# GRU layer with residual, one core: the input weights as one load over 128 rows each, x turned by each fourth column, and a new order of early loads

## The chip, the cores and the metric

The kernel runs on one core of a Trainium2 chip. The metric is the device time of one execution in microseconds (us). The time of the kernel before is the median of three runs; a few per mille of it are at stake here, so times are given to a hundredth.

## What is computed

x is 64 sequences of 128 steps with 512 features; the state h has 512 features. Each gate has a weight of 1024 rows: the first 512 meet x (the input weights), the last 512 meet the state (the state weights). All is float32.

```
def step(h, inp):
    x_t, prop = inp
    comb = jnp.concatenate([x_t, h], axis=-1)
    z = jax.nn.sigmoid(comb @ Wz + bz)
    r = jax.nn.sigmoid(comb @ Wr + br)
    comb2 = jnp.concatenate([x_t, r * h], axis=-1)
    h_cand = jnp.tanh(comb2 @ Wh + bh)
    h_new = (1.0 - z) * h + z * h_cand
    h_next = jnp.where(prop, jnp.tanh(h_new @ Wp + bp), h_new)
    return (h_next, h_new)
```

prop is true at each fourth step but the last. The output is x plus h_new of every step.

## The kernel before

**Layout.** The batch is cut into two halves h of 32. A tile of x or of the state has 128 partitions: partition 32q+b holds, for sequence b of a half, the quarter q (128 features) of the vector. VectorE's transpose works on 32x32 blocks. `join_x` (L254 to 263) turns one step of x, so that partition 32q+e then holds, in slot k, feature 128q+32k+e for all sequences. The weights stand to match: `load_w` (L98 to 103) loads rows 128q+32k to 128q+32k+31 to partitions 32q to 32q+31, slot k, with one DMA for each q, that is 4 DMAs of 32 partitions, on two queues by turns (SyncE's, SP, and ScalarE's, ACT). The input weights lie in one tile, wx; the state weights in wh[0] to wh[2] (r, z, h) and wp.

**Two kinds of products on TensorE.** All are recorded at L218. The products of the state with wh and wp are the recurrence: step t needs step t-1. The products of x with wx (`fill`) depend on no state; they stand in a queue of units, from which the code takes a counted number at set places of each step (`PLACES`, `HEAD`, `TAIL`, L613 to 620), so that TensorE has work while the gates are computed. Steps 0 to 3 take plain products. Later steps are done in groups of four by a scheme with fewer products, for which GpSimd (POOL) forms sums of rows of x (`sum_raw12` and the like, L330 to 359) and of parts of wx (`sum_outer`, `sum_inner`), and joins the results into cp (L564 to 570).

**One step** (`half`, L817 to 906; both halves run interleaved): gate r; sigmoid of r on ScalarE; r*h on VectorE (L834) and its turn (L835, recorded at L247); gate z; sigmoid of z; keep = (z-1)*h on VectorE (L850); gate h with r*h; tanh; two VectorE operations (L873, L882) and the turn of the new state (L883), with which the next step begins. `seed` copies the x part into a gate's accumulator (ScalarE, L394). `join(t, duo, u, n)` (L724) turns steps of x at two places of a step: n=0 stands behind the turn of r*h of the second half (L841), n=1 behind keep (L853). The loop repeats every 8 steps; u counts them, and duo is the round.

**The start** (L120 to 142 and L632 to 674), in the order written: steps 0 and 1 of x (step 1 on GpSimd's queue), wx for r in two parts, the biases, wx for z, wx for h, the initial state; 48 small products that only keep TensorE busy (`idle`, L633); turns of steps 0 and 1; the x products of r for both steps; then steps 2 and 3 of x and wh of r; the x products of z, then wh of z; the x products of h, then wh of h; then x for steps 4 to 11, wp and more x (`later_loads`). Then 6 units of step 2, and the recurrence.

Each queue issues in order. An issue of SP or ACT takes one of eight completion semaphores by turns, and waits until the load that had it eight places earlier in the common order of both queues has landed. On ACT an issue that waits also holds up the copies and sigmoids behind it. In the program built from it, TensorE's first product with a weight waits for all parts of that weight.

Of the kernel before, what the change touches and what calls it, by code (L numbers as in the profile page):

```python
# [18 lines left out]
def kernel(  # L19
# [14 lines left out]
    nc = tc.nc  # L34
    B, T, D = x.shape
# [7 lines left out]
    K = D // P  # L43
# [4 lines left out]
    R, Z, H_ = range(3)  # L48
# [22 lines left out]
    wx = const.tile([P, K, 3, H], F32, name="wx")  # L71
# [10 lines left out]
    gates_in = (Wr, Wz, Wh)  # L82
# [5 lines left out]
    def part(q):  # L88
        return slice(q * V, (q + 1) * V)
# [8 lines left out]
    def load_w(wt, w, k0=0, k1=K, engs=(nc.sync, nc.sync)):  # L98
        for q in (0, 2, 1, 3):
            engs[q // 2].dma_start(  # L100
                out=wt[part(q), k0:k1, :],
                in_=w[q * P + k0 * V : q * P + k1 * V, :].rearrange("(k e) n -> e k n", e=V),
            )

    both_queues = (nc.sync, nc.scalar)
# [6 lines left out]
    def load_step(t, engs=both_queues):  # L112
        for q in (0, 2, 1, 3):
            engs[q // 2].dma_start(
                out=xr[0][part(q), t], in_=x[:, t, ts(q, J)].rearrange("(h b) u -> b h u", h=S)
            )

    software_queue = (nc.gpsimd, nc.gpsimd)

    h_init = two.tile([P, S, J], F32, tag="h", name="h_init")  # L120
    bias_x = const.tile([P, C, S, 3, J // 2], F32, name="bias_x")
    bias_p = const.tile([P, S, J], F32, name="bias_p")
    new_xr(0)
    load_step(0)
    load_w(wx[:, :, R, :], gates_in[R][:D], 0, 2, both_queues)
    load_step(1, software_queue)
    for i, b in enumerate((br, bh, bz)):
        nc.gpsimd.dma_start(out=bias_row[:, i, :], in_=b.rearrange("(o n) -> o n", o=1))
    load_w(wx[:, :, R, :], gates_in[R][:D], 2, K, both_queues)

    dummy = const.tile([1, 1], F32, name="dummy")
    nc.scalar.activation(dummy, ones[:, 0:1], AF.Sigmoid)

    for i in (Z, H_):
        load_w(wx[:, :, i, :], gates_in[i][:D], engs=both_queues)

    held = const.tile([1, 1], F32, name="held")
    nc.gpsimd.tensor_copy(held, wx[0:1, 2, R, 0:1])
    for h in range(S):
        nc.gpsimd.dma_start(  # L140
            out=h_init[:, h, :],
            in_=h0[ts(h, V), :].rearrange("b (q j) -> q b j", q=NQ),
        )

    def load_wh(i):
        load_w(wh[i], gates_in[i][D:], engs=both_queues)
# [107 lines left out]
    def join_x(g, i):  # L254
        if g * Q4 >= T:
            return
        if g not in xT:
            xT[g] = xtp.tile([P, Q4, C, P], F32, tag="xT", name=f"xT_{g}")
        src = xr[g] if g < FIRST else xs[g]
        nc.vector.transpose(  # L260
            out=xT[g][:, i].rearrange("p c (a h b) -> p h (c a) b", a=S, h=S),
            in_=src[:, i].rearrange("p h (k e) -> p h k e", k=K),
        )

    def outer(kb, nb, ka):
# [29 lines left out]
    def sum_outer(n):  # L295
        for ka in range(S):
            if n == 3:
                nc.gpsimd.tensor_sub(tw[3][:, ka], outer(1, 1, ka), outer(0, 1, ka))
            elif n == 2:
                nc.gpsimd.tensor_add(tw[2][:, ka], tw[3][:, ka], outer(0, 0, ka))  # L300
            else:
                nc.gpsimd.tensor_sub(tw[4][:, ka], outer(1, 0, ka), tw[2][:, ka])
# [27 lines left out]
    def sum_raw12(g):  # L330
        v = xT[g]
        sx[g, 12] = one.tile([P, 4, C, B], F32, tag="s12r", name=f"s12r_{g}")
        four([sx[g, 12][:, n] for n in range(4)], v[:, 0], v[:, 1])
# [19 lines left out]
    def sum_s34(g):  # L353
        v = xT[g]
        o = sx[g, "o34"] = one.tile([P, 2, 2, P], F32, tag="o34", name=f"o34_{g}")
        nc.gpsimd.tensor_sub(o[:, 0], v[:, 0:2, 0, :], v[:, 2:4, 0, :])
        nc.gpsimd.tensor_sub(o[:, 1], v[:, 0:2, 1, :], sx[g, "o12"][:, 1])
        s = sx[g, 73] = one.tile([P, 4, 2, B], F32, tag="s73", name=f"s73_{g}")
        four([s[:, n] for n in range(4)], o[:, :, 0], o[:, :, 1])
# [31 lines left out]
    def seed(i, t, h):  # L391
        if t < T:
            rows = slice(None) if i == Z else ts(h, 2 * V)
            nc.scalar.copy(  # L394
                gate_ps(i, h)[rows].rearrange("p d (c n) -> p d c n", c=C),
                G[t][rows, :, :, i, :].rearrange("p c d n -> p d c n"),
            )
# [181 lines left out]
    def outer_1(g):  # L579
        with_bias(g, 1, bias0)  # L580

    def outer_c11(g):
        add(c_block(g, 0, 0), m_(g, 1), m_(g, 2))
# [14 lines left out]
    def outer_c22(g):  # L598
        add(c_block(g, 1, 1), m_(g, 7), m_(g, 5))

    def outer_c21(g):
        add(c_block(g, 1, 0), m_(g, 7), m_(g, 4))

    def pair_left(a, p1, p2, g=1):
        with_bias(g, p2, bias0)
        add(c_block(g, a, 0), m_(g, p1), m_(g, p2))

    def pair_right(a, p1, x_, g=1):
        with_bias(g, x_, bias_x[:, 1])
        add(c_block(g, a, 1), m_(g, p1), m_(g, x_))  # L610
# [17 lines left out]
    def now(units):  # L628
        put(units)
        both(len(units))  # L630
# [7 lines left out]
    spread(scratch[3], slice(0, 2), (R, H_))  # L638
    spread(scratch[1], slice(2, 3), (Z,))
    nc.gpsimd.tensor_sub(bias_d, bias_x[:, 1], bias0)  # L640
    load_step(2)
    now(first[R][0][2:] + first[R][1][2:])
    for t in range(2):
        add_bias(t, (R,))
    for h in range(S):
        seed(R, 0, h)
    load_step(3)
    load_wh(R)
    now(sum(first[Z], []))
    for i in (1, 2):  # L650
        sum_inner(i, nc.vector, slice(0, 2))
# [72 lines left out]
    def join(t, duo, u, n):  # L724
        even, odd = FIRST + 2 * duo, FIRST + 2 * duo + 1
        if t == 1:
            join_x(1, 2 + n)
        elif t == 2:
            join_x(2, n)
        elif t == 4:  # L730
            join_x(3, 2 * n)
            join_x(3, 2 * n + 1)
        elif duo >= 0 and u in (5, 6):
            join_x(even + 2, 2 * (u - 5) + n)
        elif duo >= 1 and u in (1, 3):
            join_x(odd, u - 1 + n)

    def behind_step(t, duo, u, h_new):
        g, j = divmod(t, Q4)
        even, odd = FIRST + 2 * duo, FIRST + 2 * duo + 1  # L740
        if t == T - 7:
            pair_left(0, 1, 2, LAST)
            pair_right(0, 1, 10, LAST)
        if t == 0:
            sum_outer(2)
            sum_outer(4)
        if t == 3:
            pair_left(1, 8, 9)
            pair_right(1, 8, 11)

        if duo >= 0:
            if u == 0 and duo >= 1 and odd - 2 < LAST:
                outer_c22(odd - 2)
                outer_c21(odd - 2)
            if even * Q4 < T:
                if u == 0:
                    sum_s34(even)
                elif u == 1:
                    outer_1(even)
                    outer_c11(even)  # L760
                    sum_raw12(odd)
                elif u == 2:
                    outer_u1(even)
                    outer_5(even)
                    sum_raw4(even)
                elif u == 3:
                    outer_c12(even)
                    outer_u2(even)
                    outer_c22(even)
                    if odd < LAST:  # L770
                        sum_s12(odd)
                elif u == 4:
                    if odd < LAST:
                        sum_s34(odd)
                    outer_c21(even)
                    if odd < LAST:
                        outer_1(odd)
                elif u == 5 and odd < LAST:
                    sum_raw4(odd)
                elif u == 6 and odd < LAST:  # L780
                    outer_u1(odd)
                    outer_c11(odd)
                elif u == 7 and odd < LAST:
                    outer_5(odd)
                    outer_c12(odd)
        if duo >= -1 and (even + 2) * Q4 < T:
            if t == 2 or (u == 6 and duo >= 0):
                sum_raw12(even + 2)
            if u == 7:
                sum_s12(even + 2)  # L790
        if t < T - 1:
            nc.gpsimd.tensor_add(xr[g][:, j], xr[g][:, j], h_new)  # L792

        n = 0
        if t >= T - CHUNK:
            n = 3 if t == T - 2 else 0
        elif j == Q4 - 1:
            n = 4
        if n:
            for h in range(S):  # L800
                for q in range(NQ):
                    nc.sync.dma_start(  # L802
                        out=out[ts(h, V), t - n + 1 : t + 1, ts(q, J)],
                        in_=xr[g][part(q), j - n + 1 : j + 1, h, :],
                    )
        if j == 1 and g >= 1 and (g + 1) * Q4 < T:
            new_xr(g + 1)
            load_x(xr[g + 1], (g + 1) * Q4, Q4)
        if t in (1, 2):
            load_xs(t + 2)  # L810
        if duo >= 0:
            if u == 3:
                load_xs(odd + 2)
            elif u == 6:
                load_xs(even + 4)

    def half(h):  # L817
# [95 lines left out]
    while any(live):  # L913
        h = 0 if live[0] and (not live[1] or at[0] <= at[1]) else 1
# [46 lines left out]
```

## Time and profile before

| | |
|---|---|
| median of 3 runs | 1269.17 us (1269.16 to 1270.07) |
| the profiled execution's own time | 1271.65 us |
| its span on the core | 1269.8 us |
| TensorE products busy | 1251.8 us (99%), 25960 instructions |
| VectorE busy | 772.3 us (61%) |
| ScalarE busy | 835.7 us (66%) |
| GpSimd busy | 893.1 us (70%) |
| DMA | 60.82 MB, mean 48 GB/s |

The profile is of one execution. Its own time is 1.85 us more than its span, and 2.48 us more than the median of the runs. PE is TensorE's products, PEld its weight loads, DVE VectorE, ACT ScalarE, POOL GpSimd, SPq, ACTq and POOLq the issues of DMAs on these engines. In a row of the timeline stand start, busy time, engine, line, operation and, in brackets, how long the engine was idle before it and what ended that. In a row of stretches stand, for each engine, busy time and instructions, then the clock granted to TensorE (1.00 is full), the share of the 16 DMA engines' time that was busy, and GB/s.

### The profile page before, as it was taken

Reading aid. Unit: us, or ns where it says so; the run is one execution under the profiler, and the core shown is the slowest. Engines: PE = TensorE matmul, PEld = TensorE weight load, DVE = VectorE, ACT = ScalarE, POOL = GpSimd, SP = SyncE. Lnnn points to the kernel's source line nnn. Section 1 sums busy time; section 2 is a strip of 40 time slices with the busy share of each in tenths; the row PEclk is TensorE's granted clock in tenths of the full one; section 3 lists DMA queues with packets and bytes.
Section 4 is the critical chain, followed back from the end, with each engine's and each line's share of the span. In section 5 each row is a group of like instructions: output and inputs, shape, how many; then the busy total and the mean of one; then the engine's idle time right before and its main releaser. Section 6 shows DMA issues by size and latency. Waiting matters only on the chain.

```text
span 1269.8 us, 60717 instructions
## 1 busy us (share of the span) xinstructions
PE 1251.8 (99%) x25960; PEld 1164.5 (92%) x25960; DVE 772.3 (61%) x2165; ACT 835.7 (66%) x2685; POOL 893.1 (70%) x1036
## 2 busy tenths in 40 slices
PE   7999999999999999999999999999999999999997
PEld 4898899999999999999999999999999999999875
DVE  3565666666666666666666666666666666665554
ACT  1466666666666666667666667666666766667665
POOL 3889767787677777767787677786777687677530
PEclk9999999999999999999999999999999999999999
DMA  9401222111121111212101121111111112111010
GB/s 212 109 15 48 53 52 51 38 32 43 51 53 36 43 46 36 53 38 62 38 24 52 53 52 37 36 44 45 52 37 49 40 36 53 44 45 36 9 46 19
DMA packets 113172, 60.82 MB, mean 48 GB/s; under 512 B 12968, under 2 KB 109224, under 8 KB 112904
## 3 DMA queue, kind: packets, MB, share of 16 engines
q1 hardware_dynamic: 110148, 53.26, 16.3%
q8 instruction: 205, 3.36, 1.2%
q10 hardware_dynamic: 2372, 3.41, 1.2%
q14 instruction: 63, 0.52, 0.1%
q0 software_dynamic: 384, 0.27, 0.1%
HBM read 40.11 MB, written 16.78 MB: 45 GB/s over the span
## 4 chain that ended last, share of the span: by engine, by line
PE 92%; POOL 2%; DMA 2%; issue 1%; ACT 1%; DVE 1%; SPq 0%; ACTq 0%; POOLq 0%; DVEq 0%
PE rec L218 42%; PE rec_z L218 15%; PE scratch_r L218 13%; PE scratch_q L218 10%; PE scratch_a L218 5%; PE scratch_y L218 4%; PE scratch_x L218 4%; DMA wx<-in_L_cond_Wh_dram 1%; POOL cp L565 1%; POOL mb L570 1%; DMA wh<-in_L_cond_Wr_dram 0%; DMA xr<-in_x_dram 0%; DMA wx<-in_L_cond_Wr_dram 0%; ACT rec_z L244 0%; SPq L802 0%
## 5 line engine op out<-in xcount | busy, mean ns | idle before, releaser
L218 PE MATMUL rec<-wh,rhT 128*32 128x256 f32 x4096 | 375.4, 379 | 0.1
L218 PE MATMUL rec<-wh,hT 128*32 128x256 f32 x3072 | 281.5, 379 | 1.3 <-DVE hT L247 1.3
L218 PE MATMUL rec_z<-wh,hT 128*32 128x256 f32 x3072 | 281.7, 379 | 0.1
L218 PEld LDWEIGHTS rec<-wh,rhT 128*32 128x32 f32 x4096 | 250.1, 110 | 19.2 <-ACT scratch_r L244 0.5
L244 ACT ACTIVATE scratch_r<-rec 64x128 f32<-64x128 f32 x512 | 128.0, 250 | 137.6 <-PE rec L218 64.0
L394 ACT COPY rec<-cp 64x256 f32<-64x256 f32 x512 | 189.8, 371 | 27.1 <-DMA xr<-in_x_dram 7.6
L218 PEld LDWEIGHTS rec_z<-wh,hT 128*32 128x32 f32 x3072 | 192.4, 110 | 9.7 <-ACT rec_z L394 0.6
L218 PEld LDWEIGHTS rec<-wh,hT 128*32 128x32 f32 x3072 | 186.4, 110 | 14.7 <-ACT c L244 3.2
L244 ACT ACTIVATE rec_z<-rec_z 64x128 f32<-64x128 f32 x512 | 128.0, 250 | 98.1 <-PE rec_z L218 86.0
L244 ACT ACTIVATE c<-rec 64x128 f32<-64x128 f32 x512 | 139.3, 272 | 60.1 <-PE rec L218 48.6
L792 POOL TENSOR_TENSOR xr<-xr,h 128x256 f32<-128x256 f32 x127 | 92.9, 732 | 93.0 <-DVE h L882 93.0
L565 POOL TENSOR_TENSOR mb<-mb,mb 128x768 f32<-128x768 f32 x58 | 106.2, 1830 | 67.0 <-DVE mb L531 67.0
L565 POOL TENSOR_TENSOR cp<-mb,mb 128x768 f32<-128x768 f32 x76 | 138.8, 1827 | 8.1 <-DVE mb L531 4.4
L565 POOL TENSOR_TENSOR cp<-mb 128x768 f32<-128x768 f32 x46 | 84.2, 1831 | 56.9 <-ACT rec_z L394 55.5
L850 DVE SCALAR_TENSOR_TENSOR keep<-rec_z,h 128x256 f32<-128x256 f32 x96 | 40.8, 425 | 133.7 <-ACT rec_z L244 127.4
L218 PE MATMUL scratch_r<-tw,s 128*32 128x192 f32 x928 | 120.9, 326 | 0.0
L504 ACT COPY cq<-scratch_q 128x384 f32<-128x384 f32 x212 | 102.1, 482 | 19.7 <-PE scratch_q L218 18.3
L521 DVE TENSOR_TENSOR cx<-scratch_r,cx 128x384 f32<-128x384 f32 x106 | 59.1, 557 | 81.4 <-PE scratch_r L218 70.1
L218 PE MATMUL scratch_q<-tt,s 128*32 128x192 f32 x928 | 103.6, 326 | 0.0
L527 DVE TENSOR_TENSOR mb<-scratch_q,cx 128x384 f32<-128x384 f32 x106 | 59.1, 557 | 57.8 <-ACT cq L504 57.6
L834 DVE TENSOR_TENSOR rh<-scratch_r,h 128x128 f32<-128x128 f32 x192 | 56.0, 292 | 60.3 <-ACT scratch_r L244 60.3
L218 PE MATMUL rec<-wh,hpT 128*32 128x256 f32 x992 | 91.5, 379 | 0.1
(184 smaller groups left out, 3819.9 us busy)
## 6 DMA issues: line engine op xcount, KB each, us to landing
out_dram<-xr SPq DMA_DIRECT2D x249, 64.0 KB, 1.8
xr<-in_x_dram SPq DMA_DIRECT2D x248, 64.0 KB, 2.1
xs<-in_x_dram SPq DMA_DIRECT2D x240, 64.0 KB, 2.2
wp<-in_L_cond_Wp_dram SPq DMA_DIRECT2D x4, 256.0 KB, 5.0
wx<-in_L_cond_Wr_dram SPq DMA_DIRECT2D x4, 128.0 KB, 3.6
wx<-in_L_cond_Wr_dram ACTq DMA_DIRECT2D x4, 128.0 KB, 4.1
wx<-in_L_cond_Wz_dram ACTq DMA_DIRECT2D x2, 256.0 KB, 5.9
wx<-in_L_cond_Wz_dram SPq DMA_DIRECT2D x2, 256.0 KB, 6.6
```

What stands on the lines that cost most here:

```text
L218: nc.tensor.matmul(ps[part(2 * h + c)], lhsT=left, rhs=rhs(c), start=start, stop=True, skip_group_check=True,)
L244: nc.scalar.activation(dst[ts(d, 2 * V)], gate_ps(i, h)[ts(h, 2 * V), d, :], func)
L394: nc.scalar.copy(gate_ps(i, h)[rows].rearrange("p d (c n) -> p d c n", c=C), G[t][rows, :, :, i, :].rearrange("p c d n -> p d c n"),)
L504: nc.scalar.copy(c[:, :nm], ps[:, :nm])
L521: nc.vector.tensor_add(T2[what][:, :nm], r_ps[:, :nm], T2[what][:, :nm])
L527: nc.vector.tensor_add(blocks(1, 1), runs(q_ps[:, :nm]), runs(T2[what][:, :nm]))
L565: nc.gpsimd.tensor_add(dst, a, b)
L570: nc.gpsimd.tensor_add(m, m, v.unsqueeze(1).to_broadcast([P, 2, 3 * J]))
L792: nc.gpsimd.tensor_add(xr[g][:, j], xr[g][:, j], h_new)
L834: nc.vector.tensor_mul(rh[:, h, :], r_, h_old[:, h, :])
L850: nc.vector.scalar_tensor_tensor(out=keep, in0=z, scalar=1.0, in1=h_old, op0=ALU.subtract, op1=ALU.mult)
```

## The change

- wx is loaded by a new `load_wx`: one DMA over 128 partitions for each gate, two for r (slots 0 and 1, then 2 and 3), all on SP's queue. Partition p holds in slot k row 4p+k of the weight.
- `join_x` reads x to match: within a quarter, the 32 columns e of slot k are each fourth column, 4e+k, where they were 32 neighbours.
- Step 1 of x goes from GpSimd's queue to ACT's. Step 2 (all on ACT's) is issued ahead of the initial state, where it stood behind the first x products of r. Step 3 goes to ACT's queue.
- wh of r takes the place in the order that step 2 had, ahead of step 3, where it stood behind step 3.
- In the loop the joins with n=1 go; their turns stand with n=0, behind the turn of r*h, in part a step later: u=5 one turn, u=6 one, u=7 two; and u=1 two, u=2 one, u=3 one. Before it was two in each of u=5, 6, 1 and 3, one at each place.
- The load of the next even group of x follows at u=7, where it followed at u=6.

```diff
+    def load_wx(i, k0, k1):
+        nc.sync.dma_start(
+            out=wx[:, k0:k1, i, :],
+            in_=gates_in[i][:D].rearrange("(p k) n -> p k n", k=K)[:, k0:k1],
+        )
...
     load_step(0)
-    load_w(wx[:, :, R, :], gates_in[R][:D], 0, 2, both_queues)
-    load_step(1, software_queue)
+    load_wx(R, 0, 2)
+    load_step(1, (nc.scalar, nc.scalar))
...
-    load_w(wx[:, :, R, :], gates_in[R][:D], 2, K, both_queues)
+    load_wx(R, 2, K)
...
     for i in (Z, H_):
-        load_w(wx[:, :, i, :], gates_in[i][:D], engs=both_queues)
+        load_wx(i, 0, K)
+    load_step(2, (nc.scalar, nc.scalar))
...
-            in_=src[:, i].rearrange("p h (k e) -> p h k e", k=K),
+            in_=src[:, i].rearrange("p h (e k) -> p h k e", k=K),
...
-    load_step(2)
+    load_wh(R)
     now(first[R][0][2:] + first[R][1][2:])
...
-    load_step(3)
-    load_wh(R)
+    load_step(3, (nc.scalar, nc.scalar))
...
-        elif duo >= 0 and u in (5, 6):
-            join_x(even + 2, 2 * (u - 5) + n)
-        elif duo >= 1 and u in (1, 3):
-            join_x(odd, u - 1 + n)
+        elif n == 0:
+            if duo >= 0 and u in (5, 6):
+                join_x(even + 2, u - 5)
+            elif duo >= 0 and u == 7:
+                join_x(even + 2, 2)
+                join_x(even + 2, 3)
+            elif duo >= 1 and u == 1:
+                join_x(odd, 0)
+                join_x(odd, 1)
+            elif duo >= 1 and u in (2, 3):
+                join_x(odd, u)
...
-            elif u == 6:
+            elif u == 7:
                 load_xs(even + 4)
```

More of the change, by code (lines that the diff above doesn't have):

```diff
@@ L116, in load_step @@
             )
-    software_queue = (nc.gpsimd, nc.gpsimd)
+    def load_wx(i, k0, k1):
[3 more added lines that the diff above has]
+        )
     h_init = two.tile([P, S, J], F32, tag="h", name="h_init")
```

## The prediction

> **What bounds the kernel now.** The stretches of the windows view come first, because an average hides that this kernel has three parts.
>
> ```profile
> span 1269.8 us, 60717 instructions
> 0.00:28.50 28.50, 20.32 (x304) 10.69 (x304) 11.52 (x31) 3.53 (x8) 8.39 (x19) 1.00 0.89 210
> 28.50:60.00 31.50, 31.42 (x590) 25.64 (x594) 15.62 (x46) 14.82 (x49) 28.85 (x29) 0.95 0.53 122
> 60.00:110.00 50.00, 48.91 (x1059) 46.52 (x1053) 28.80 (x79) 29.48 (x92) 41.23 (x48) 1.00 0.18 45
> 510.00:710.00 200.00, 200.00 (x4204) 190.49 (x4199) 126.43 (x355) 137.48 (x442) 145.19 (x168) 1.00 0.18 47
> 710.00:910.00 200.00, 200.00 (x4219) 191.39 (x4215) 126.08 (x353) 136.93 (x440) 147.33 (x177) 1.00 0.17 45
> ```
>
> The first column after the stretch is its length, the next TensorE's busy time. From 510 to 910 TensorE is busy for 400.00 of 400.00 us at clock 1.00: nothing that another engine gains there can shorten it. The change leaves the products and their order alone (as many of them, line for line, in both programs). So the loop can only lose. At the start it is otherwise: 8.2 us of 28.50 are idle, and the DMA engines are busy for 0.89 of their time. The waits of TensorE and its timeline name the holes.
>
> ```profile
> PE rec L218 <- DMA wh<-in_L_cond_Wr_dram: 3.2, 1, 3.2
> PE scratch_r L218 <- DMA xr<-in_x_dram: 1.9, 1, 1.9
> PE scratch_a L218 <- DVE xT L260: 1.0, 1, 1.0
> ...
> 15.23 1.94 PE L218 MATMUL scratch_a<-wx,xT 128*32 128x256 f32 x32
> 19.12 1.93 PE L218 MATMUL scratch_r<-wx,xT 128*32 128x256 f32 x32 [1.95 <-DMA xr<-in_x_dram]
> ...
> 22.57 2.80 PE L218 MATMUL scratch_q<-wx,xT 128*32 128x256 f32 x48
> 28.58 2.74 PE L218 MATMUL rec<-wh,hT_init 128*32 128x256 f32 x28 [3.21 <-DMA wh<-in_L_cond_Wr_dram]
> ```
>
> In order: the x products of z end at 17.17; those of h begin at 19.12, when wx of h is there (scratch_r is their accumulator; the x named as releaser was issued together with it); they and six units of step 2 run to 25.37; then TensorE stands until 28.58 for r's state weights (wh of r). The recurrence begins there, and everything after it moves with it.
>
> The hole has a second price, in the clock.
>
> ```profile
> 29.80:33.20 3.40, 3.40 (x40) 2.23 (x34) 0.60 (x2) 1.42 (x5) 3.24 (x5) 0.53 1.08 216
> 33.20:36.00 2.80, 2.80 (x60) 2.08 (x55) 1.24 (x4) 1.06 (x4) 2.80 (x3) 1.00 0.57 108
> ```
>
> Right after the hole the granted clock is 0.53 for 3.4 us, and only 40 products run. At the rate of the next stretch (60 in 2.80 us) 40 take 1.87 us: 1.5 us lost.
>
> **The change part by part.**
>
> *wh of r sooner.* Its loads were issued late.
>
> ```profile
> 11.55 2.52 SPq L114 DMA_DIRECT2D xr<-in_x_dram  x4
> 17.55 2.38 SPq L100 DMA_DIRECT2D wh<-in_L_cond_Wr_dram  x2
> ...
> 15.02 4.19 ACTq L114 DMA_DIRECT2D xr<-in_x_dram  x2
> 19.30 0.49 ACTq L114 DMA_DIRECT2D xr<-in_x_dram  x1
> 20.31 2.32 ACTq L100 DMA_DIRECT2D wh<-in_L_cond_Wr_dram  x2
> ...
> 15.00:18.00 3.00, 2.17 (x42) 1.26 (x32) 2.79 (x9) 0.00 (x0) 0.00 (x0) 1.00 1.00 230
> 18.00:21.00 3.00, 1.88 (x36) 1.44 (x40) 0.24 (x2) 0.74 (x2) 0.00 (x0) 1.00 0.63 135
> ```
>
> They stood behind steps 2 and 3 of x, each of which waits for a semaphore of a load still under way, and the DMA engines fell from 230 to 135 GB/s meanwhile. In the new order SP's two parts wait only for the second part of wx of r and for the first part of step 2, ACT's two for the last part of step 1 and for wx of z. All four waits end before wx of h has landed, so wh of r lies in the queue when the engines come free. Its 1 MB at 230 GB/s takes 4.6 us behind wx of h (about 18.9): landed near 23.5, while TensorE is at work until 25.37. I take the whole 3.2 us as gone; cover left 1.9 us, and beyond it each us late costs one us. What waits behind: on ACT the copies that seed r, the third part of step 3 (which now waits for all of wx of h), the seed of z, wh of z and of h, then the first sigmoid of r; all have until 25 to 34, as below.
>
> *The half clock.* If TensorE goes on from 25.37 without a hole, the 1.5 us go too. Bounds: 0 (another hole brings it) and 1.6 (the stretch's 3.40 x 0.47).
>
> *wx as one load of 128 partitions, all from SP; step 1 of x on ACT's queue.* As many bytes and rows of 2 KB; 12 issues of about 0.3 to 0.5 us become 4 on SP. No row shows an input weight loaded so. The stretches bound what could be gained:
>
> ```profile
> 1.50:3.00 1.50, 1.50 (x20) 0.61 (x16) 0.00 (x0) 0.00 (x0) 1.50 (x3) 1.00 0.50 106
> 3.00:4.50 1.50, 1.50 (x20) 0.53 (x16) 0.29 (x1) 0.12 (x1) 1.50 (x4) 1.00 0.89 259
> 12.00:15.00 3.00, 2.45 (x48) 1.43 (x44) 2.29 (x6) 0.00 (x0) 0.74 (x1) 1.00 1.08 199
> ```
>
> Between 106 and 259 GB/s there is room for a steeper start; from 3 us on the engines are full. The best case for wx of h is that nearly all of the wait of 1.9 us vanishes, say 1.7 (more can't, since z's x products end at 17.17); the worst, that half of step 2, now ahead of it (0.06 MB, 0.3 us at 230 GB/s), and slower work of one queue make it 1.0 later. I take 0.4 us earlier. The wait of 1.0 us for step 1 is worth nothing either way: z's weights and then h's are waited for behind it.
>
> *x turned by each fourth column.* No row has such a read.
>
> ```profile
> L260 DVE STREAM_TRANSPOSE xT<-xs 128x256 f32<-128x256 f32 x120 | 51.2, 429 | 2.2 <-issue 0.4
> L306 DVE TENSOR_TENSOR d<-wx 128x768 f32<-128x768 f32 x2 | 1.8, 932 | 0.0
> ```
>
> Bounds: 0.43 us as now, and 0.93 us, as a pass over three times the columns. I take 0.43, the same instruction. In the start the turns of steps 0, 2 and 3 lie under weights still in flight; in the loop the next rows say what hides them.
>
> *Joins behind the turn of r\*h.* The tightest place is u=7, where two turns come together:
>
> ```profile
> 692.53 0.31 DVE L247 STREAM_TRANSPOSE rhT<-rh 128x128 f32<-128x128 f32 x1
> 693.88 0.42 DVE L850 SCALAR_TENSOR_TENSOR keep<-rec_z,h 128x256 f32<-128x256 f32 x1 [1.04 <-ACT rec_z L244]
> 694.51 0.29 DVE L873 TENSOR_TENSOR rec_z<-c,rec_z 128x128 f32<-128x128 f32 x1 [0.21 <-ACT c L244]
> ...
> 695.24 0.31 DVE L247 STREAM_TRANSPOSE hT<-h 128x128 f32<-128x128 f32 x1
> 695.97 0.41 PE L218 MATMUL rec<-wp,hT 128*32 128x256 f32 x2
> ```
>
> VectorE is idle for 1.04 us ahead of keep, so two turns of 0.43 fit and keep is not late. Cost 0. If turns grow, 0.21 us of idle time ahead of L873 and 0.42 us between the end of hT (695.55) and its use (695.97) come on top: 1.67 us for two, 0.83 each, before TensorE waits.
>
> *Behind the start.* If the recurrence begins 5 us sooner, what is late next?
>
> ```profile
> 35.44 0.41 PE L218 MATMUL rec_z<-wh,hT_init 128*32 128x256 f32 x2
> 39.56 1.29 PE rec L218 x24
> ...
> 40.61 0.46 POOL L325 TENSOR_TENSOR s12r<-xT 128x128 f32<-128x128 f32 x1 [2.02 <-DVE xT L260]
> 67.97 0.46 POOL L325 TENSOR_TENSOR s12r<-xT 128x128 f32<-128x128 f32 x1 [7.43 <-PE scratch_r L218]
> ```
>
> wh of z is wanted at 35.44 - 5 = 30, wh of h at 34.5. Each is 1 MB: after 23.5, step 3 and these at 4.6 us each land near 28 and 33. GpSimd's start may stay where it is: it has 2.0 and 7.4 us to give up to 67.97, where TensorE releases it. So the gain is kept.
>
> The sum: 3.2 + 1.5 + 0.4 = 5.1 us. Against the profiled execution: 1271.65 - 5.1 = 1266.55; its time is 2.48 above the median, and I take the same terms for the other runs: 1269.17 - 5.1 = **1264.1 us**.
>
> **The rivals.**
>
> 1. *The half clock comes elsewhere.* TensorE still stands between 17.17 and about 18.7; were it to stand for 3 us there, half speed would fall on h's x products. Against: before, 1.9 us there brought none. Then 3.2 + 0.4 = 3.6: 1265.6. The Trainium skill, TensorE: Matmul & The Clock Gate, Part 1, "What's actually happening", says that the clock is halved after an idle window of about 3.4 us that runs freely, so the same hole may or may not cost; the trace agrees in the length of the slow stretch (3.4 us at 0.53), and by that rule the chance of this rival is not small.
>
> 2. *wh of r takes bandwidth from wx of h.* If the queues share, ACT's half (0.5 MB, 2.2 us at 230) goes beside it: h's products begin 2.2 - 0.4 = 1.8 us later at 20.9, the hole ahead of them grows to 3.7 and brings the half clock there. The recurrence begins at 25.37 + 1.8 + 1.5 = 28.7, 0.1 late, and 1.5 are saved behind it: gain 1.4, 1267.8. Against it:
>
> ```profile
> wh<-in_L_cond_Wr_dram SPq DMA_DIRECT2D x1, 256.0 KB, 4.3
> xr<-in_x_dram ACTq DMA_DIRECT2D x2, 32.0 KB, 4.0
> ```
>
> Issued together (19.3 to 20.3), two loads of 32 KB on ACT's queue took as long as one of 256 KB on SP's: they land in order of issue, not by shares of the queues.
>
> 3. *Slower: the turns by each fourth column stall the loop.* The point is 0.83 us a turn (above). At 1.25 us, three times now, a pair at u=7 is 2.5 - 1.67 = 0.83 us too long; 120 turns are 15 rounds, so 12.5 us: 1264.1 + 12.5 = 1276.6. Faster turns to slower at (5.1/15 + 1.67)/2 = 1.0 us. The Trainium skill, SBUF — State Buffer, "Door 1: The DMA port swizzle", speaks for it: memory lines are 16 bytes, and each access that crosses to a new line pays; each fourth float does so every time. No row here has such a read.
>
> **How the numbers follow.** Forecast 0.60; rival 1 0.15; rival 2 0.12; rival 3 0.09; that the change brings almost nothing, because ACT's waits hold wh of r back as before, 0.04 (near 1269). A measurement of this kernel can tell about 0.2% from no change, 2.5 us: faster is below 1266.6. The forecast and rival 1 lie below it, as does 0.02 of rival 2: faster 0.77; same 0.10 + 0.04 = 0.14; slower 0.09. The range takes the best of all terms, 3.2 + 1.6 + 1.7 = 6.5 (1262.7), and the worst without rival 3: 3.2 + 0 - 1.0 = 2.2 (1267.0).
>
> **What would show it.** The first product of rec with wh at 24.2 to 25.6 and no wait for wh of r; clock 1.00 from 25 to 36; the wait ahead of scratch_r 1 to 2 us; turns at 0.43 us; 200 of 200 us busy from 510 on. It is wrong if wx of h lands after 20, if the clock falls anywhere, or if TensorE is idle in the loop behind hT.

## The result, and the profile after

After: **1265.95 us** median (1264.16 to 1266.38, 7 runs); before in the same session 1269.17 (1268.55 to 1272.09, 7 runs). The ratio is 0.9967, 95% interval 0.9955 to 0.9978: faster by 3.2 us, inside the range 1262.7 to 1267.0 and 1.85 us above the forecast. The profiled execution took 1266.30 us, its span 1264.5. The gain is 3.2 of the 5.1 us that were forecast; the experiments show that it comes for the most part from another place than the prediction said.

The stretches of after, columns as before:

```profile
span 1264.5 us, 60718 instructions
0.00:28.50 28.50, 24.61 (x372) 12.06 (x374) 12.76 (x33) 5.28 (x14) 6.97 (x16) 0.94 0.88 237
28.50:60.00 31.50, 31.50 (x656) 24.21 (x650) 19.42 (x51) 15.94 (x52) 28.60 (x28) 1.00 0.44 109
60.00:110.00 50.00, 48.93 (x1050) 44.16 (x1043) 29.93 (x80) 30.33 (x96) 46.20 (x50) 1.00 0.15 39
510.00:710.00 200.00, 200.00 (x4206) 192.26 (x4201) 132.08 (x353) 136.57 (x439) 144.61 (x167) 1.00 0.17 46
710.00:910.00 200.00, 200.00 (x4218) 192.26 (x4213) 130.66 (x352) 136.64 (x440) 148.65 (x173) 1.00 0.16 42
```

The loop is as it was (200 of 200 us, as many products to within two). From 28.5 to 60 the clock is 1.00 in place of 0.95. In the first stretch it is 0.94 in place of 1.00: the half clock has moved there. The timeline of TensorE in after:

```profile
5.24 0.39 PE L213 MATMUL rec_z<-zeros 128*32 128x512 bf16 x4
6.83 1.07 PE L223 MATMUL scratch_q<-wx,xT 128*32 128x256 f32 x16 [1.20 <-DMA wx<-in_L_cond_Wr_dram]
9.38 1.07 PE L223 MATMUL scratch_a<-wx,xT 128*32 128x256 f32 x16 [1.49 <-DVE xT L265]
10.39 1.06 PE L195 MATMUL scratch_x<-tt,ones 1*32 1x512 f32 x8
11.27 0.94 PE L195 MATMUL scratch_r<-tt,ones 1*32 1x256 f32 x8
12.14 1.94 PE L223 MATMUL scratch_q<-wx,xT 128*32 128x256 f32 x16
...
15.20 1.90 PE L223 MATMUL scratch_q<-wx,xT 128*32 128x256 f32 x32
...
18.65 1.90 PE L223 MATMUL scratch_r<-wx,xT 128*32 128x256 f32 x32
...
24.70 1.93 PE L223 MATMUL rec<-wh,hT_init 128*32 128x256 f32 x28
```

Rec begins at 24.70 in place of 28.58. Neither h's x products nor rec wait: from 9.38 on TensorE runs without a hole. But its clock is halved from 11.4 to 14.8 (16 products take 1.94 us there, at full clock 1.07), and so TensorE itself has become the bound of the start. From the first product of rec to the end: 1264.5 - 24.70 = 1239.8 us; before 1269.8 - 28.58 = 1241.2, of which 1.5 were the half clock at 29.8. So 3.9 + 1.4 = 5.3 us were gained in the profiles.

The loads show why nothing waits for weights any more behind 9.38. Stretches of before:

```profile
6.00:9.00 3.00, 1.65 (x28) 0.78 (x28) 0.45 (x1) 0.00 (x0) 1.52 (x3) 1.00 1.09 248
9.00:12.00 3.00, 3.00 (x52) 1.16 (x44) 0.00 (x0) 0.92 (x3) 0.26 (x1) 1.00 1.07 240
```

The same stretches of after, and a later one in which state weights arrive:

```profile
6.00:9.00 3.00, 1.07 (x16) 0.50 (x16) 0.30 (x1) 0.00 (x0) 0.28 (x2) 1.00 1.07 385
9.00:12.00 3.00, 2.62 (x32) 0.82 (x32) 0.33 (x1) 0.49 (x2) 1.23 (x2) 0.90 1.02 344
18.00:21.00 3.00, 3.00 (x60) 1.68 (x56) 2.93 (x10) 0.00 (x0) 0.00 (x0) 1.00 0.87 185
```

At an engine share of 1.0 to 1.1 in both, the load over 128 partitions moves 344 to 385 GB/s, the loads over 32 partitions 240 to 248. These are the rates of these stretches: from 24 to 27, where before has only loads over 32 partitions under way, it reaches 298 at a share of 1.03. wx of h has landed at 16.5; before at 18.9.

The price is on VectorE. The turns of x in the loop, by shape, in after:

```profile
L265 DVE STREAM_TRANSPOSE xT<-xs 128x256 f32<-128x256 f32 x120 | 74.4, 641 | 1.9
```

641 ns in place of 429, within the bounds given and under the stall point of 0.83 us.

### The profile page after: what moved, and what is told of

It reads as the page before. It is cut to its first block, busy times and chain, and to the rows that moved or that the text cites. A ratio compares the mean times of both kernels' runs of the same rounds, so it can differ in the third digit from the quotient of the medians.

```text
span 1264.5 us, 60718 instructions
## 1 busy us (share of the span) xinstructions
PE 1250.6 (99%) x25960; PEld 1161.0 (92%) x25960; DVE 803.9 (64%) x2165; ACT 835.2 (66%) x2685; POOL 891.1 (70%) x1032
## 4 chain that ended last, share of the span: by engine, by line
PE 94%; POOL 2%; issue 1%; DMA 1%; ACT 1%; DVE 1%; SPq 0%; ACTq 0%; POOLq 0%; DVEq 0%
PE rec L223 42%; PE rec_z L223 16%; PE scratch_r L223 13%; PE scratch_q L223 10%; PE scratch_a L223 5%; PE scratch_x L223 4%; PE scratch_y L223 4%; DMA xr<-in_x_dram 1%; POOL cp L570 1%; POOL mb L575 1%; ACT rec_z L249 0%; SPq L813 0%; POOL xr L803 0%; ACT c L249 0%; DVE rec_z L884 0%
## 5 line engine op out<-in xcount | busy, mean ns | idle before, releaser
L223 PEld LDWEIGHTS rec<-wh,hT 128*32 128x32 f32 x3072 | 186.2, 110 | 14.6 <-ACT c L249 2.7
```

The lines of the kernel that those rows point to most:

```text
L223: nc.tensor.matmul(ps[part(2 * h + c)], lhsT=left, rhs=rhs(c), start=start, stop=True, skip_group_check=True,)
```

## The experiments

All twelve in one table. They ran in three groups, e1 to e4, e5 to e8 and e9 to e12, each with before beside it, so kernels of different groups are best compared by their ratios. The first product of rec and the time from there to the end of the span are those of the profiled execution; medians are of 6 to 12 runs, ratios against before in the same group (1270.3 to 1270.7 us).

| kernel | median (range) us | ratio, 95% interval | first rec | rest |
|---|---|---|---|---|
| before | 1269.17 (1268.55 to 1272.09) | 1 | 28.58 | 1241.2 |
| after | 1265.95 (1264.16 to 1266.38) | 0.9967, 0.9955 to 0.9978 | 24.70 | 1239.8 |
| e12_control (after again) | 1265.71 (1264.83 to 1269.60) | 0.9966, 0.9955 to 0.9978 | 23.52 | 1239.9 |
| e1_order_only | 1270.66 (1269.74 to 1271.79) | 1.0002, 0.9994 to 1.0011 | 28.87 | 1239.5 |
| e5_order_behind_copies | 1269.41 (1267.91 to 1270.41) | 0.9989, 0.9981 to 0.9998 | 26.21 | 1239.7 |
| e2_wx_only | 1268.86 (1267.45 to 1272.24) | 0.9993, 0.9983 to 1.0003 | 26.16 | 1242.3 |
| e6_joins_as_before | 1270.60 (1269.14 to 1273.38) | 1.0006, 0.9996 to 1.0016 | 26.43 | 1242.4 |
| e11_no_order | 1266.21 (1265.07 to 1270.05) | 0.9973, 0.9964 to 0.9982 | 25.13 | 1239.6 |
| e3_step1_both | 1269.20 (1267.09 to 1270.46) | 0.9988, 0.9979 to 0.9997 | 27.13 | 1239.9 |
| e4_idle | 1264.99 (1264.30 to 1270.47) | 0.9964, 0.9953 to 0.9974 | 29.23 | 1239.5 |
| e8_idle_one_queue | 1266.33 (1265.80 to 1269.86) | 0.9970, 0.9960 to 0.9979 | 24.31 | 1240.1 |
| e7_wh_r_one_queue | 1267.61 (1264.76 to 1269.64) | 0.9979, 0.9970 to 0.9988 | 22.68 | 1240.2 |
| e9_bias_early | 1266.19 (1263.61 to 1271.14) | 0.9968, 0.9956 to 0.9980 | 25.18 | 1239.8 |
| e10_bias_early_wh_later | 1265.01 (1263.70 to 1270.36) | 0.9961, 0.9948 to 0.9974 | 24.95 | 1239.8 |

### Which part brings the gain

**e1_order_only**, against before:

```diff
     for i in (Z, H_):
         load_w(wx[:, :, i, :], gates_in[i][:D], engs=both_queues)
+    load_step(2, (nc.scalar, nc.scalar))
...
-    load_step(2)
+    load_wh(R)
...
-    load_step(3)
-    load_wh(R)
+    load_step(3, (nc.scalar, nc.scalar))
```

> The kernel before with the order of the loads alone changed: step 2 of x is issued on ScalarE's queue right behind the input weights, r's state weights at the place where step 2 was, step 3 on ScalarE's queue. Input weights in four loads of 32 partitions over both queues, turns, joins and step 1 of x as before. Theory A (the order does the work): no wait for wh of r, the first product of rec at about 25.4, the wait of 1.9 us ahead of scratch_r still there, no half clock behind the start of rec: 1269.17 - 3.2 - 1.5 = about 1264.5 us. Rival B (the single load does the work, since the quarters keep ScalarE's queue busy): the wait for wh of r stays at 2 us or more and the time at 1267 to 1269 us.

No gain: 1270.66, with before at 1270.31 in its group, so that B's 1267 to 1269 is missed as well as A's time. Neither mechanism came: nothing waits for wh of r, whose last part landed at 25.6. ScalarE and its queue in e1:

```profile
9.44 6.62 ACTq L114 DMA_DIRECT2D xr<-in_x_dram  x4
16.10 0.65 ACT L200 COPY bias_x<-scratch_x 128x256 f32<-128x256 f32 x2 [10.66 <-DMA wx<-in_L_cond_Wh_dram]
```

and TensorE in e1:

```profile
16.99 3.64 PE L220 MATMUL scratch_q<-wx,xT 128*32 128x256 f32 x32 [4.49 <-DVE cp L434]
```

Step 2's four issues hold ScalarE for 6.6 us, since each waits for its semaphore, the last until a part of wx of h is there. The copies of the biases stand behind them, VectorE needs these to free the accumulator, and z's products begin at 16.99 (before 13.51), at half clock after the hole. With 4 loads of wx in place of 16 the semaphores come round to step 2 sooner: in after these copies are at 11.51, and nobody waits.

**e5_order_behind_copies**: e1 with step 2 issued behind the copies.

```diff
-    load_step(2, (nc.scalar, nc.scalar))
...
     spread(scratch[1], slice(2, 3), (Z,))
     nc.gpsimd.tensor_sub(bias_d, bias_x[:, 1], bias0)
+    load_step(2, (nc.scalar, nc.scalar))
     load_wh(R)
```

> The order of the loads alone, as in e1_order_only, but with step 2 of x issued on ScalarE's queue behind the copies of the biases in place of ahead of them. Theory G (in e1 the gain of the order was eaten by ScalarE: its issue of step 2 waited for weights under way, the copies of the biases stood behind it until 16.1, and TensorE waited 4.5 us for what VectorE made of them): that wait is under 1 us, z's x products begin near 13.5, wh of r lands near 23 to 24, first product of rec at 25 to 26.3, 1265.5 to 1267.5 us. Rival H (it is not the place on ScalarE but the quarter loads on two queues that cost it): 1269.5 us or more.

The 4.5 us hole is gone and rec begins at 26.21, as G has it, although the half clock now falls on 11.3. wh of r has landed at 26.0 (before 28.4, G 23 to 24), inside a last wait ahead of rec (the x named as its releaser was issued right behind wh of r):

```profile
26.21 1.96 PE L218 MATMUL rec<-wh,hT_init 128*32 128x256 f32 x28 [0.49 <-DMA xr<-in_x_dram]
```

The median, 1269.41, misses G's range and nearly is H's: the profiled run was the fastest of eleven, and why the others took 1.5 us more is not known. By its ratio the order alone is worth 1.4 us (0.2 to 1.9 per mille), not 4.7.

**e2_wx_only**, against before, with `load_wx` as in after:

```diff
-    load_w(wx[:, :, R, :], gates_in[R][:D], 0, 2, both_queues)
+    load_wx(R, 0, 2)
...
-    load_w(wx[:, :, R, :], gates_in[R][:D], 2, K, both_queues)
+    load_wx(R, 2, K)
...
-        load_w(wx[:, :, i, :], gates_in[i][:D], engs=both_queues)
+        load_wx(i, 0, K)
...
-            in_=src[:, i].rearrange("p h (k e) -> p h k e", k=K),
+            in_=src[:, i].rearrange("p h (e k) -> p h k e", k=K),
```

> The kernel before with the input weights alone changed: one load over 128 partitions, on SyncE's queue, and x turned by each fourth column; step 1 of x on GpSimd's queue, steps 2 and 3, r's state weights and the joins as before. Theory A: wx of h lands about 2 us sooner and the wait ahead of scratch_r is gone, but wh of r is still issued behind steps 2 and 3, so that TensorE waits for it all the same: first product of rec at 27 to 28.5, 1267.5 to 1269.2 us. Rival B: with the queues free wh of r comes soon enough although it is issued late: first product of rec at 25, 1265 us.

The time is A's, the mechanism B's: nothing waits for wh of r although it is issued behind steps 2 and 3. With only the loads of wx changed, the stretch from 9 to 12 us moves 404 GB/s in place of 240:

```profile
9.00:12.00 3.00, 2.84 (x32) 0.91 (x32) 0.10 (x1) 0.35 (x2) 0.57 (x1) 0.79 1.05 404
```

Two things ate the gain: 1242.3 us from rec to the end, 2.5 more than after; and in this execution a half clock of 6.8 us, from 10.7 on.

**e6_joins_as_before**, against after:

```diff
-        elif n == 0:
-            if duo >= 0 and u in (5, 6):
-                join_x(even + 2, u - 5)
...
+        elif duo >= 0 and u in (5, 6):
+            join_x(even + 2, 2 * (u - 5) + n)
+        elif duo >= 1 and u in (1, 3):
+            join_x(odd, u - 1 + n)
```

> The kernel after with the turns of x in the loop at their places of before (half of them behind keep). Theory J (the turn by each fourth column takes 0.65 us in place of 0.43, and behind keep it makes the turn of h late, by some 0.17 us in each of 15 rounds; behind the turn of r*h it does not): from the first product of rec to the end of the span 1242 to 1242.6 us in place of 1239.8, the median 2 to 3 us above the kernel after, 1268 to 1269 us. Rival K (the 2.5 us that e2_wx_only lost there came from its loads or its step 1): within 0.5 us of the kernel after, 1265.5 to 1266.4 us.

J's time behind rec came: again 1242.4. VectorE in e6, at one of the two places in a round of 77 us where it shows:

```profile
664.69 0.42 DVE L854 SCALAR_TENSOR_TENSOR keep<-rec_z,hprop 128x256 f32<-128x256 f32 x1 [0.93 <-ACT rec_z L249]
665.03 0.66 DVE L265 STREAM_TRANSPOSE xT<-xs 128x256 f32<-128x256 f32 x1
665.63 0.26 DVE L877 TENSOR_TENSOR rec_z<-c,rec_z 128x128 f32<-128x128 f32 x1
665.99 0.29 DVE L886 TENSOR_TENSOR h<-rec_z,keep 128x128 f32<-128x128 f32 x1
666.31 0.31 DVE L252 STREAM_TRANSPOSE hT<-h 128x128 f32<-128x128 f32 x1
```

The same place in after:

```profile
660.15 0.69 DVE L265 STREAM_TRANSPOSE xT<-xs 128x256 f32<-128x256 f32 x1
661.74 0.42 DVE L861 SCALAR_TENSOR_TENSOR keep<-rec_z,hprop 128x256 f32<-128x256 f32 x1 [0.89 <-ACT rec_z L249]
662.31 0.30 DVE L884 TENSOR_TENSOR rec_z<-c,rec_z 128x128 f32<-128x128 f32 x1
662.71 0.29 DVE L893 TENSOR_TENSOR h<-rec_z,keep 128x128 f32<-128x128 f32 x1
663.04 0.31 DVE L252 STREAM_TRANSPOSE hT<-h 128x128 f32<-128x128 f32 x1
```

From the start of keep to the end of hT: 1.93 us in e6, 1.61 in after, because the longer turn stands between them. TensorE covers part of that; 2.5 us over 15 rounds, 0.17 a round, stay. The round itself, from this keep to the same one a round later, takes 77.05 us in e6 and 76.87 in after. The turn grew by 0.2 us, and the move of the joins is what pays for it. (The median of e6 is 4.7 us above after's, where J had 2 to 3. In the profiles the difference is 4.3; the part that is not behind rec lies in the start, with half clock from 11.3 to 18.1.)

**e11_no_order**: after with the order of the small loads and of wh of r as before.

```diff
-    load_step(1, (nc.scalar, nc.scalar))
+    load_step(1, (nc.gpsimd, nc.gpsimd))
...
-    load_step(2, (nc.scalar, nc.scalar))
...
-    load_wh(R)
+    load_step(2)
...
-    load_step(3, (nc.scalar, nc.scalar))
+    load_step(3)
+    load_wh(R)
```

> The kernel after with the order of the small loads and of r's state weights as before: step 1 of x on GpSimd's queue, steps 2 and 3 over both queues ahead of wh of r. One load for wx, turns by each fourth column and the joins behind the turn of r*h stay. Theory N (with the input weights in four loads in place of twelve the queues come free so soon that wh of r is in time even behind steps 2 and 3, as in e2_wx_only, where it landed at 22.7 and nothing waited for it): from the first product of rec to the end 1239.5 to 1240.2 us, the first product at 22.8 to 26.2 according to the half clock, the median 1264.8 to 1266.6, within 0.7 us of e12_control. Rival, the forecast's own view (issuing wh of r sooner is worth 3.2 us by itself): wait for wh of r ahead of rec, 1267.5 us or more.

N came: 1266.21, 0.5 us from the control, with the intervals on top of each other. TensorE in e11:

```profile
22.54 2.77 PE L224 MATMUL scratch_q<-wx,xT 128*32 128x256 f32 x48
25.13 1.93 PE L224 MATMUL rec<-wh,hT_init 128*32 128x256 f32 x28
```

No wait ahead of rec. SyncE's and ScalarE's queues in e11 issue wh of r at 15.5 to 17.2, in before at 17.55 to 22.6; it has landed at 22.7 against 28.4. **So the load over 128 partitions and the move of the joins make the gain between them; the new order adds nothing that can be measured, and without the new load it is worth 1.4 us or, as in e1, nothing.** The new load differs from the old in four ways at once: 128 partitions in place of 32, the rows 4p+k, 4 loads in place of 16, and one queue in place of two. No run takes these apart.

### The half clock and the early waits

**e3_step1_both**, against after:

```diff
-    load_step(1, (nc.scalar, nc.scalar))
+    load_step(1)
```

> The kernel after with step 1 of x on both queues (two parts ahead of the second part of wx of r on SyncE's queue) in place of four parts on ScalarE's. Theory C (TensorE's early wait of 1.5 us comes from step 1 landing behind the second part of wx of r): the wait is gone or under 0.4 us, the second half of r's x products begins 1.0 to 1.5 us sooner, and the first product of rec at 23.2 to 23.7 (22.6 if the half clock goes with it): 1264.0 to 1264.9 us, beside 1265.95 of the kernel after. Rival D (the start is bound by the bytes of the weights, not by step 1): first product of rec at 24.3 or later, 1265.5 to 1266 us.

Step 1's wait falls to 0.46 us, near C's 0.4, but the median is 3.5 us above the control's (2.2 per mille by the ratios): C's time fails, and D's too. TensorE's waits in e3:

```profile
PE scratch_r L223 <- DMA wx<-in_L_cond_Wh_dram: 3.5, 1, 3.5
PE scratch_q L223 <- DMA wx<-in_L_cond_Wz_dram: 1.6, 1, 1.6
```

Two more issues on SyncE's queue put wx of z out at 6.90 in place of 4.60, and the stretch from 6 to 9 us moves 200 GB/s in place of 385. One wait was exchanged for a later and longer one.

**e4_idle**, against after:

```diff
-    idle(48)
+    idle(58)
...
     join_x(0, 1)
+    idle(14)
     now(first[R][1][:2])
```

> The kernel after with 58 in place of 48 products of zeros ahead of the first x product, and 14 more between the products of step 0 and those of step 1, so that TensorE does not stand still in the two early waits (1.2 and 1.5 us). Theory E (these two holes together bring the half clock at 11.4): clock 1.00 from 6 us on, first product of rec at 23.1 to 23.6, and 1264.4 to 1264.9 us in every run; the scatter of the kernel after from 1264.2 to 1266.4 shrinks. Rival F (the half clock has another cause, or full speed in the middle only makes TensorE wait for the weights): first product of rec within 0.4 us of 24.7, 1265.5 to 1266.4 us.

**e8_idle_one_queue**, against e4:

```diff
-        load_w(wh[i], gates_in[i][D:], engs=both_queues)
+        load_w(wh[i], gates_in[i][D:], engs=(nc.sync, nc.sync) if i == R else both_queues)
```

> e4_idle (58 and 14 products of zeros in the early waits) and e7 together. Theories E and L: no half clock ahead of 25, none of the late runs that e4_idle had (1269.2 and 1270.5 of 12), 1264.2 to 1265.0 us in all runs, median 1264.6. Rival M: late runs as in e4_idle, median above 1265.

**e9_bias_early**, against after:

```diff
     join_x(0, 1)
-    now(first[R][1][:2])
     spread(scratch[3], slice(0, 2), (R, H_))
     spread(scratch[1], slice(2, 3), (Z,))
     nc.gpsimd.tensor_sub(bias_d, bias_x[:, 1], bias0)
+    now(first[R][1][:2])
```

> The kernel after with the products that spread the biases (1.4 us of TensorE) ahead of the x products of step 1 in place of behind them, so that they fall into the wait for step 1's turn. Theory P (the half clock at 11.4 follows a stretch of 3.4 us with too little TensorE work in it, and the wait of 1.5 us ahead of step 1 is the larger part of it): the wait is under 0.3 us, the second half of r's x products begins at 10.4 to 10.8 in place of 12.1, no half clock in the profile, the first product of rec at 22.4 to 23.2, and a median of 1264.0 to 1265.0. Rival Q (wx of h decides, and what TensorE does ahead of 16 does not matter): the half clock comes now and then as before, and the median is within 0.5 us of e12_control.

e4's profile has no half clock at 11.4, but it caught one of the late executions (wx of h at 20.2, and the half clock behind that wait); the scatter did not shrink. In e8 the half clock came all the same, and in e9, which filled the wait for step 1 as meant, sooner and for 6.8 us: E and P both fail. Q's time came (e9 is 0.5 us from the control), which by itself does not show Q's reason. The stretches are cut at the clock's own steps of 3.41 us. Of e8:

```profile
8.00:11.40 3.40, 2.87 (x41) 0.82 (x32) 0.63 (x1) 0.28 (x2) 1.50 (x3) 1.00 1.05 344
11.40:14.80 3.40, 3.40 (x36) 1.58 (x36) 0.42 (x1) 1.39 (x5) 0.99 (x1) 0.50 1.07 300
```

Of e9:

```profile
5.80:9.20 3.40, 2.30 (x32) 0.78 (x28) 0.12 (x1) 0.00 (x0) 0.24 (x2) 1.00 1.06 376
9.20:12.60 3.40, 3.40 (x36) 1.38 (x32) 0.52 (x1) 1.02 (x3) 2.27 (x3) 0.50 1.06 360
```

Of before:

```profile
5.70:9.10 3.40, 2.05 (x36) 0.82 (x32) 0.45 (x1) 0.17 (x1) 1.52 (x3) 1.00 1.07 247
9.10:12.50 3.40, 3.40 (x56) 1.43 (x52) 0.27 (x1) 0.92 (x3) 0.76 (x1) 1.00 1.07 242
```

e8's window is busy for 2.87 us of 3.40 and is followed by half speed; before's with 2.05 is not. e8's holds 16 x products and 16 one-row products that spread the biases, before's 28 x products and a few of zeros. In the fourteen profiles every window of the start at full clock that half speed followed held 12 to 20 products with 128 rows, apart from at most four of zeros; none that held 23 or more was followed by it. The number alone does not decide it: in e11 the first window at full clock (from 5.5) held 16 and four of zeros and full clock followed, while in e9 the first window (from 5.8) held the same with nine one-row products besides, and half clock followed. Still, one-row products seem to count little or nothing; that was seen, not tried by itself. The Trainium skill, TensorE: Matmul & The Clock Gate, Part 1, "What's actually happening", has the window right (free-running, about 3.4 us; the slow stretches here are 3.41 or 6.83 us) but speaks of an idle window; here windows busy for 2.02 us (after, from 8.0) and 2.87 us (e8) were followed by half speed. Where the windows begin differs from run to run (full clock came between 3.9 and 7.1 us), so the same program has the half clock in some runs: e12's profile, of the same kernel, has none, and full clock came there at 7.07, in after's at 4.59. After's three with a mean clock of 0.997 took 1265.98 to 1266.38, the other four 1264.16 to 1265.95.

### What makes wx of h late

**e7_wh_r_one_queue**: after with the edit of e8.

> The kernel after with r's state weights in four loads on SyncE's queue, behind wx of h, and none on ScalarE's. Theory L (what ScalarE's half of wh of r sends beside wx of h makes the last of its sixteen parts land late, 16.5 in the profile of after and 20 to 21 in those of e3 and e4, and so scatters the runs): the wait ahead of scratch_r is 0 to 0.5 us in the profile, runs between 1264 and 1266.4, none at 1267 or more. Rival M (the late parts come from the chip's side, whatever stands on the other queue): runs up to 1268 to 1270 as in e4, the median at 1266 or above.

**e10_bias_early_wh_later**, against e9:

```diff
-    load_wh(R)
     now(first[R][0][2:] + first[R][1][2:])
...
         seed(R, 0, h)
+    load_wh(R)
     load_step(3, (nc.scalar, nc.scalar))
```

> e9_bias_early with r's state weights issued a little later: behind the seeds of r in the program, so that ScalarE's two parts go out at about 13 and not at 10 to 12. Theory R (ScalarE's half of wh of r, sent beside wx of h, makes the last sixteenth of wx of h late, most where it went out first: 10.5 in e3, 11.9 in e4, 12.3 in after): wx of h all landed by 16.5, runs between 1263.5 and 1265.5, less scatter than e9. Rival S (wh of r is then itself late): a wait ahead of rec of 0.5 to 1.5 us, the median 0.5 to 1.5 us above e9.

**e12_control**:

> The kernel after, unchanged, run again beside these three: 1265.0 to 1266.4 us, the first product of rec at 22.6 to 24.8 according to the half clock. It shows how much of a difference between the other runs is the chip's.

A load counts as landed when the last of its sixteen parts is there. Of wx of h, in after, twelve parts land from 13.2 to 13.8 and the last at 16.5. L fails: e7's profile is the earliest of all (rec at 22.68), and its median 1.9 us above the control. M's figures came, with runs up to 1269.6 in e7 and 1269.9 in e8, but where the late parts come from is not seen. R's forecast fails too, though e10 hardly tests it: ScalarE's parts went out at 12.05 and 12.41, later than in e9 (10.34) but not later than in after (12.26 and 12.62). TensorE waits in e10

```profile
PE scratch_r L223 <- DMA wx<-in_L_cond_Wh_dram: 3.1, 1, 3.1
```

for a last part at 18.8, and not for wh of r as S has it. Where wh of r was issued only after wx of h had landed (e2, e11), the last part came at 15.0 and 14.6; in the other runs with one load from 15.8 to 21.0. That would fit wh of r as the cause, which is rival 2's mechanism. But in e2 and e11 wx of h itself was issued sooner, at 4.5 in place of 7.6 to 8.8, and from issue to landing it took 10.5 and 10.1 us there, 7.6 to 13.3 in the others. So the cause stays open, and with it the scatter of several us in the runs of e4, e7, e9, e10. e4 and e10 have medians 0.7 us below the control, within the scatter: no version here is shown to beat after.

## Why the prediction was right, and where not

- **Wait for wh of r (3.2): the size right, the cause wrong.** The wait is gone, and wh of r landed at 22.3 (forecast 23.5). But the term does not hang on the step "They stood behind steps 2 and 3 of x": in e11 they still stand there, and there is no wait (landed at 22.7); with the order alone the last part landed at 26.0 and 0.5 us of the wait stayed (e5), and most of the gain failed to come (e1, e5). The loads of wx (16, not the 12 of the prediction; now 4) held the semaphores and the engines; which of the two weighed more is not shown. What waits behind ACT's issues was listed for wh of r, and the copies of the biases behind step 2 left out; e1 shows what they cost, 4.5 us.
- **wx of h (0.4): mis-sized.** "From 3 us on the engines are full" took a busy share of 0.9 to 1.1 for a full rate. Equally busy engines moved 240 to 248 GB/s with the old loads and 344 to 404 with the new, in the stretches shown. The whole wait of 1.9 us went. The Trainium skill, SBUF — State Buffer, "Door 1: The DMA port swizzle" and, further on, "Can I just issue two DMAs to hit both halves?", states a rule that would explain it: partitions 0 to 31 reach 8 of 16 ports, only one load over all 128 reaches 16, and two loads at a time do not make up for it. The trace agrees in the direction (e2 against before: 404 to 240 GB/s), but rows, number and queue changed with the partitions; the prediction took from "Door 1" only the 16-byte lines.
- **The half clock (1.5): rival 1, at another place.** It is gone at 29.6 and came at 11.4, in some runs. It was looked for ahead of h's products, where the hole was; it followed a window of 3.4 us in which step 1's wait (1.5 us in place of 1.0, since its last part lands with wx of r's second) and the one-row products left 16 x products. The step "The wait of 1.0 us for step 1 is worth nothing either way" overlooked that; as a wait alone it was right (e3, e10).
- **Turns (0.43): mis-sized inside the bounds,** 0.64. Rival 3 did not come: 0.64 is under 0.83. "Cost 0" for the moved joins was right as far as it went, but their worth was missed: at their old places the longer turns cost 2.5 us.
- **Behind the start:** right. From rec to the end 1239.8, before 1239.7 without its half clock; wh of z, of h and GpSimd were in time.
- **The sum:** 5.1 forecast, 5.3 in the profiles, 3.2 between the medians. "I take the same terms for the other runs" failed: before's profiled execution lay 2.5 us above its median, after's 0.35, and what differs between executions is these very terms. That the time fell inside the range is in part luck: most of the wait and of wx of h's 1.9 us came from a load that was given 0.4, and the half clock at 11.4 took some of it back. Rival 1's 1265.6 lies nearer, within 0.35, but it too has the 3.2 us from the order.

## What to carry to other kernels

A DMA share near 1 says that the engines are busy, not that they move what they can: compare GB/s between loads of different shapes, and try one that spans all 128 partitions. When a change has several parts, ask of each what it does without the others: here a load, a dearer turn and a move of turns only paid together, and the part that looked like the cause was not needed. A term read from one execution's start is a term of that execution; take the clock and the landings from several.

## What the runs showed of the hardware

- Stretches of 3 us with loads of wx of 512 KB to 1 MB over 128 partitions moved 344 to 404 GB/s in after and e2 (300 in e10 from 9 to 12); stretches with loads over 32 partitions on two queues 240 to 248 in before (298 from 24 to 27). The engines were equally busy in all, a share of 1.0 to 1.1. Whether the partitions do it, or the rows (4p+k, neighbours in memory), the number of loads or the queue, was not tried.
- VectorE's turn of 128x256 float32 with each fourth column read takes 0.64 to 0.66 us, with neighbours 0.43.
- In the start, each window of 3.41 us at full clock that half clock followed held 12 to 20 products of 128 rows beside at most four of zeros, and TensorE was busy for up to 2.87 us of it. Not every such window was followed by half clock (e11, from 5.5).
